# Sparse graph attention on one core: more slots in two chunks, the sum in the first slot's buffer, and ScalarE's first part put one or two tiles later

## The chip, the cores and the metric

The kernel runs on one core of a Trainium2 chip. The metric is the device time of one execution in microseconds (us). The core has five engines that work side by side: TensorE (PE, with its weight loads shown apart as PEld), VectorE (DVE), ScalarE (ACT), GpSimd (POOL) and SyncE (SP). The last three also issue transfers, which 16 DMA engines carry out. Each engine takes its instructions in a fixed order and waits on semaphores for the others.

## The reference

One layer of graph attention over N = 3327 nodes with D = 1024 features, with a residual. The adjacency is a dense int32 matrix, but almost all of it is zero.

```python
h = jnp.maximum(_layernorm(x, axis=-1), 0.0)
f = h @ Wf + bf
g = h @ Wg + bg
e = jax.nn.relu(f @ g.T)
scores = jnp.where(adj > 0, e, -9e15)
attention = jax.nn.softmax(scores, axis=1)
out = x + attention @ (h @ W + bW)
```

## The kernel before

The kernel does not compute all scores. **Part 1** reads the adjacency in 26 tiles of 128 rows, makes for each row a list of its neighbours (at most 40) and their number (the degree), writes the layer-normed rows h to DRAM (`hd`) and the lists to DRAM (`pd`), and builds A = Wf Wg^T, so that a row's scores against its neighbours are dots of q = h A with the neighbours' rows of h. Then the rows are ranked by degree, highest first, and `perm` holds the order. **Part 2** takes 128 ranked rows at a time. Such a group is called a slot s here, and `CAPS[s]` is how many neighbours its rows may have. For every k below the cap, one indirect transfer gathers 128 rows of h, each the k-th neighbour of its row.

```python
CAPS = [37, 25, 23, 22, 21, 21, 20, 20, 19, 19, 18, 18, 17, 17, 17, 16, 16, 15, 15, 15, 14, 14, 13, 13, 12, 11]
ONE_CHUNK = 20
AHEAD = 3
LAG = 4
```

Part 1, one tile. Odd tiles take their mean and variance on VectorE, even ones on ScalarE:

```python
def normed(t):
    ...                                   # xt: 128 rows of x, loaded
    if t % 2:
        ...                               # L406: two bn_stats, bn_aggr -> mv
        nc.scalar.activation(nmr[:n], mv[:n, 0:1], AF.Copy, scale=-1.0)            # L409
        nc.scalar.activation(rstd[:n], mv[:n, 1:2], AF.Sqrt, bias=eps[:n])         # L410
    else:
        ...                               # L414 to L418: the same with sums on ScalarE
    nc.vector.reciprocal(rstd[:n], rstd[:n])                                       # L419
    nc.scalar.activation(nmr[:n], nmr[:n], AF.Copy, scale=rstd[:n])                # L420
    nc.scalar.activation(xt[:n], xt[:n], AF.Relu, bias=nmr[:n], scale=rstd[:n])    # L421
    ...                                   # L423: xt stored to hd

def degrees(t):
    r = kpool.tile([P, N], FP, name="r")  # four buffers; the adjacency rows are loaded into it
    ...
        nc.scalar.activation(r[:n, b:e], a[:n, b:e], AF.Relu, accum_out=to)        # L435: 0/1 and degree
        nc.gpsimd.tensor_mul(r[:n, b:e], r[:n, b:e], iotaj[:n, b:e])               # L436: column numbers

def edges(t, r):
    cand = cpool.tile([P, SEG * 8], FP, name="cand")
    for s in range(SEG):                  # L446: the 8 largest of each of 16 segments
        nc.vector.max(cand[:n, s * 8 : s * 8 + 8], r[:n, s * SW : min(N, (s + 1) * SW)])
    pos = cpool.tile([P, SEG * 8], BF, name="pos")
    nc.vector.tensor_scalar(pos[:n], cand[:n], 0.0, None, op0=ALU.is_gt, op1=ALU.add,
                            accum_out=cnt[:n, t : t + 1])                          # L448: count
    for i in range(0, KM, 8):             # L452, L454: the 40 largest, in order
        nc.vector.max(lst[:n, i : i + 8], cand[:n])
        if i + 8 < KM:
            nc.vector.match_replace(cand[:n], lst[:n, i : i + 8], cand[:n], 0.0)
    nc.vector.tensor_scalar(lst[:n], lst[:n], float(N), 1.0, op0=ALU.min, op1=ALU.max)      # L455
    nc.vector.tensor_scalar(pay[:n, t, :KM], lst[:n], -1.0, None, op0=ALU.add)              # L456
    dg = cpool.tile([P, 1], FP, name="dg")
    nc.vector.tensor_scalar(dg[:n], deg[:n, t : t + 1], float(NBIN - 1), None, op0=ALU.min) # L458
    nc.vector.tensor_copy(pay[:n, t, KM : KM + 1], dg[:n])                                  # L459
    nc.vector.tensor_scalar(oh[:n, t, :], iotad[:n], dg[:n], None, op0=ALU.is_equal)        # L460

for t in range(NT):
    r = degrees(t)
    normed(t)
    edges(t, r)
    ...                                   # counts by degree, stores of lists, one of the 8 steps for A (L519)
```

Part 2. `prepare(s)` gathers the lists and rows of a slot and computes q (TensorE, L667). A slot above `ONE_CHUNK` is cut into two chunks, whose softmaxes are joined by rescaling the first sum.

```python
gpool = ctx.enter_context(tc.tile_pool(name="G", bufs=23))
ypool = ctx.enter_context(tc.tile_pool(name="y", bufs=2))

def dot(s, k):
    g = G[s, k] = gpool.tile([P, D], FP, name="G")
    gather(g, hd[:, :], e["pi"][:, k : k + 1])                # L638, POOL
    nc.vector.tensor_tensor_reduce(junk, g, q, ...)           # L684: one score per row

def softmax(s, k0, k1, last):
    ...                                   # L693 mask, L695 maximum
    if k0: ...                            # L697: joint maximum with the first chunk
    ...                                   # L699: exp and its sum
    if k0: ...                            # L702 and L703: factor al and joint sum
    if last: ...                          # L706 reciprocal, L708 al * rs (if k0), L709 sc * rs
    if k0:
        nc.scalar.activation(e["y"], e["y"], AF.Copy, scale=al)                    # L711

def on_tensor(s, k0, k1):                 # which k of the last chunk are summed on TensorE
    m = min(max(0, CAPS[s] - 13), k1 - k0 - 2)
    ...

def combine(s, k0, k1, last):
    if not k0:
        e["y"] = ypool.tile([P, D], FP, name="y")
    ...
        if k in pe:
            nc.scalar.activation(g, g, AF.Copy, scale=p)                           # L741
            sum_transposed(e, g, e["first"], False)                                # L725: 8 transposes
        elif k == 0:
            nc.scalar.activation(y, g, AF.Copy, scale=p)                           # L745
        else:
            nc.vector.scalar_tensor_tensor(y, g, p, y, op0=ALU.mult, op1=ALU.add)  # L747

def project(s): ...                       # y transposed, 16 matmuls with W (L759), copied to res (L761)

def finish(s):
    gather(e["r"], x[:, :], perm[:, s : s + 1], compute_op=ALU.add)                # res += x
    ins = nc.gpsimd.indirect_dma_start(out=out[:, :], ..., in_=e["r"], ...)        # L767: rows written out

for i, (s, k0, k1) in enumerate(units):   # units: the chunks in order
    last = k1 == CAPS[s]
    dots(s, range(k0, k1))
    if not k0 and s:
        finish(s - 1)
    softmax(s, k0, k1, last)
    if i + 1 < len(units):
        s2, a, b = units[i + 1]
        dots(s2, range(a, min(b, a + AHEAD)))
    combine(s, k0, k1, last)
    if last:
        project(s)
        if s + 2 < NT:
            prepare(s + 2)
```

The order of the instructions on each engine is made by the compiler's scheduler from this program order as a priority; it is not the order of the lines. A second, dense path runs only if a flag says that some row has more neighbours than its slot allows; it does not run with these inputs.

Of the kernel before, what the change touches and what calls it, by code (L numbers as in the profile page):

```python
# [8 lines left out]
FP = mybir.dt.float32  # L9
# [15 lines left out]
CAPS = [37, 25, 23, 22, 21, 21, 20, 20, 19, 19, 18, 18, 17, 17, 17, 16, 16, 15, 15, 15, 14, 14, 13, 13, 12, 11]  # L25
ONE_CHUNK = 20
AHEAD = 3
# [262 lines left out]
def edge_path(ctx: ExitStack, tc: tile.TileContext, x, adj, Wf, bf, Wg, bg, W, bW, out, flag):  # L290
# [45 lines left out]
    nc.gpsimd.memset(ones3, 1.0)  # L336
    bads = const.tile([P, NT + 2], FP, name="bads")
    nc.gpsimd.memset(bads, 0.0)
# [12 lines left out]
    with ExitStack() as part1:  # L351
# [3 lines left out]
        wT = pool1("wT", 2)  # L355
        ln = pool1("ln", 5)
        lnj = pool1("lnj", 1)
        kpool = pool1("key", 4)
        cpool = pool1("cand", 2)
        p_tr = pool1("p_tr", 2, space=PSUM)  # L360
# [32 lines left out]
        pre = p_c.tile([P, NBIN], FP, name="pre")  # L393

        def normed(t):

# [4 lines left out]
            rstd = ln.tile([P, 1], FP, name="rstd")  # L401
            nmr = ln.tile([P, 1], FP, name="nmr")
            if t % 2:
                st = ln.tile([P, D // CB, 6], FP, name="st")
                for c in range(D // CB):
                    nc.vector.bn_stats(st[:n, c, :], xt[:n, c * CB : (c + 1) * CB])  # L406
                mv = ln.tile([P, 2], FP, name="mv")
                nc.vector.bn_aggr(mv[:n], st[:n])
                nc.scalar.activation(nmr[:n], mv[:n, 0:1], AF.Copy, scale=-1.0)  # L409
                nc.scalar.activation(rstd[:n], mv[:n, 1:2], AF.Sqrt, bias=eps[:n])  # L410
            else:
                sums = ln.tile([P, 2], FP, name="sums")
                j = lnj.tile([P, D], BF, name="lnj")
                nc.scalar.activation(j[:n], xt[:n], AF.Copy, accum_out=sums[:n, 0:1])  # L414
                nc.scalar.activation(nmr[:n], sums[:n, 0:1], AF.Copy, scale=-1.0 / D)
                j = lnj.tile([P, D], BF, name="lnj")
                nc.scalar.activation(j[:n], xt[:n], AF.Square, bias=nmr[:n], accum_out=sums[:n, 1:2])
                nc.scalar.activation(rstd[:n], sums[:n, 1:2], AF.Sqrt, bias=eps[:n], scale=1.0 / D)  # L418
            nc.vector.reciprocal(rstd[:n], rstd[:n])  # L419
            nc.scalar.activation(nmr[:n], nmr[:n], AF.Copy, scale=rstd[:n])  # L420
            nc.scalar.activation(xt[:n], xt[:n], AF.Relu, bias=nmr[:n], scale=rstd[:n])  # L421
# [3 lines left out]
        def degrees(t):  # L425
# [13 lines left out]
            return r  # L439

        def edges(t, r):

            n = rows(t)
            cand = cpool.tile([P, SEG * 8], FP, name="cand")
            for s in range(SEG):
                nc.vector.max(cand[:n, s * 8 : s * 8 + 8], r[:n, s * SW : min(N, (s + 1) * SW)])  # L446
            pos = cpool.tile([P, SEG * 8], BF, name="pos")
            nc.vector.tensor_scalar(  # L448
                pos[:n], cand[:n], 0.0, None, op0=ALU.is_gt, op1=ALU.add, accum_out=cnt[:n, t : t + 1]
            )  # L450
            for i in range(0, KM, 8):
                nc.vector.max(lst[:n, i : i + 8], cand[:n])  # L452
                if i + 8 < KM:
                    nc.vector.match_replace(cand[:n], lst[:n, i : i + 8], cand[:n], 0.0)  # L454
            nc.vector.tensor_scalar(lst[:n], lst[:n], float(N), 1.0, op0=ALU.min, op1=ALU.max)  # L455
            nc.vector.tensor_scalar(pay[:n, t, :KM], lst[:n], -1.0, None, op0=ALU.add)  # L456
            dg = cpool.tile([P, 1], FP, name="dg")
            nc.vector.tensor_scalar(dg[:n], deg[:n, t : t + 1], float(NBIN - 1), None, op0=ALU.min)  # L458
            nc.vector.tensor_copy(pay[:n, t, KM : KM + 1], dg[:n])  # L459
            nc.vector.tensor_scalar(oh[:n, t, :], iotad[:n], dg[:n], None, op0=ALU.is_equal)  # L460

        def counted(t):
# [4 lines left out]
            nc.tensor.matmul(pre, tri, oh[:, t, :], start=(t == 0), stop=False, skip_group_check=True)  # L467
            hit = cpool.tile([P, NBIN], FP, name="hit")
            nc.vector.scalar_tensor_tensor(
# [84 lines left out]

        for t in range(NT):
            r = degrees(t)
            normed(t)
            edges(t, r)
            if t >= LAG:
# [7 lines left out]
            if t == 2 * KD:  # L567
                make_rows()
        for t in range(NT - LAG, NT):
            counted(t)  # L570
# [37 lines left out]
        nc.vector.tensor_copy(tens, ps[:, NT : 2 * NT])  # L608
        nc.vector.scalar_tensor_tensor(perm, ps[:, :NT], float(P), tens, op0=ALU.mult, op1=ALU.add)
        over = c1.tile([P, 1], FP, name="over")  # L610
# [5 lines left out]
        nc.vector.tensor_scalar(ne, deg, 1.0, None, op0=ALU.is_lt)  # L616
        nc.vector.tensor_reduce(bads[:, NT + 1 : NT + 2], ne, AX.X, ALU.max)


    W_sb = ctx.enter_context(tc.tile_pool(name="W", bufs=1)).tile([P, KD, O], FP, name="W_sb")  # L620
    nc.sync.dma_start(W_sb, W.rearrange("(k p) o -> p k o", p=P))
    psp = ctx.enter_context(tc.tile_pool(name="ps", bufs=3))
    gpool = ctx.enter_context(tc.tile_pool(name="G", bufs=23))
    hpool = ctx.enter_context(tc.tile_pool(name="hp", bufs=2))
    qpool = ctx.enter_context(tc.tile_pool(name="q", bufs=2))
    hTpool = ctx.enter_context(tc.tile_pool(name="hT", bufs=1))
    ypool = ctx.enter_context(tc.tile_pool(name="y", bufs=2))
    yTpool = ctx.enter_context(tc.tile_pool(name="yT", bufs=1))
# [8 lines left out]
    def gather(to, table, idx, **kw):  # L637
        nc.gpsimd.indirect_dma_start(  # L638
            out=to,
# [39 lines left out]
    def dot(s, k):  # L679
        e = st[s]  # L680
        g = G[s, k] = gpool.tile([P, D], FP, name="G")
        gather(g, hd[:, :], e["pi"][:, k : k + 1])
        junk = jpool.tile([P, D], BF, name="junk")
# [46 lines left out]
    def combine(s, k0, k1, last):  # L730
        e = st[s]
        if not k0:
            e["y"] = ypool.tile([P, D], FP, name="y")
        y = e["y"]
        e["first"] = True
        pe = on_tensor(s, k0, k1) if last else []
        for k in range(k0, k1):
# [6 lines left out]
            elif k == 0:  # L744
                nc.scalar.activation(y, g, AF.Copy, scale=p)  # L745
            else:
                nc.vector.scalar_tensor_tensor(y, g, p, y, op0=ALU.mult, op1=ALU.add)  # L747

    def project(s):
# [6 lines left out]
        for o in range(OH):  # L756
# [4 lines left out]
            nc.scalar.copy(r[:, o * CB : (o + 1) * CB], ps)  # L761

    def finish(s):
        e = st[s]

        gather(e["r"], x[:, :], perm[:, s : s + 1], compute_op=ALU.add)
        ins = nc.gpsimd.indirect_dma_start(  # L767
            out=out[:, :],
            out_offset=bass.IndirectOffsetOnAxis(ap=perm[:, s : s + 1] if s < N // P else final, axis=0),
            in_=e["r"],  # L770
            in_offset=None,
            bounds_check=None if s < N // P else N - 1,
            oob_is_err=s < N // P,
        )
        tc.declare_no_dep(ins.ins, group="results", reason="other rows")
# [27 lines left out]
    for i, (s, k0, k1) in enumerate(units):  # L803
        last = k1 == CAPS[s]
        dots(s, range(k0, k1))
        if not k0 and s:
            finish(s - 1)
        softmax(s, k0, k1, last)
        if i + 1 < len(units):
            s2, a, b = units[i + 1]  # L810
            dots(s2, range(a, min(b, a + AHEAD)))
        combine(s, k0, k1, last)
        if last:
# [46 lines left out]
```

## Time and profile before

| | us |
|---|---|
| median of 3 runs | 1418.14 (1415.55 to 1426.23) |
| profiled span | 1415.5, mean granted TensorE clock 0.927 |
| part 1: first to last MAX8 (L446) on VectorE | 20.7 to 267.1 |
| ranking and the first slot's q, until the first dot | 267 to 313 |
| last dot starts | 1353.2 |

In the profile's lines, an entry such as `L745` is the line of the kernel, `y<-G,sc` is the tile written and the tiles read, and `x26` is the number of instructions. A wait is written as the engine and instruction that stood still, an arrow, and what ended the wait. A gather's busy time on POOL is the time to issue it; the transfer itself is told by the DMA views, which give for G a median of 6.1 us from issue to landing.

### The profile page before, as it was taken

The page shows a single profiled execution, that of the slowest core. Times are in us where ns is not written, and L with a number is a line of the kernel's source. Part 1 is how long each engine was busy: PE and PEld are TensorE (multiplying, and loading weights), DVE is VectorE, ACT ScalarE, POOL GpSimd, SP SyncE. Part 2 cuts the span into 40 slices and gives each one's busy share as a digit, 9 for nine tenths or more (in the row PEclk, how much of TensorE's full clock was granted, in tenths as well). Part 3 has the DMA queues.
Part 4 walks back from the last instruction along what each step waited for, and adds up shares of the span by engine and source line. Part 5 has one row for each costly group of instructions (what it writes and reads, how often), then busy time and mean ns, then how long its engine had stood idle before and what let it go on. Part 6 is the DMA issues. An engine that isn't in the chain of part 4 may idle for free.

```text
span 1415.5 us, 14137 instructions
## 1 busy us (share of the span) xinstructions
PE 1172.8 (83%) x4355; PEld 684.0 (48%) x4355; DVE 1221.1 (86%) x2550; ACT 474.8 (34%) x738; POOL 876.6 (62%) x628
## 2 busy tenths in 40 slices
PE   4569998167288999999878977899999999999784
PEld 3544554044165556665545544555555555555331
DVE  4888889919979999998898788889999999999970
ACT  6666776311063244433312321222222222222110
POOL 8677777364666766775556556666667766666501
PEclk9999999578599999999989988999999999999897
DMA  9898796196678999886778667878889888888712
GB/s 370 330 356 307 294 346 229 49 361 236 227 269 289 316 315 330 282 291 224 266 284 277 192 248 265 275 233 266 256 285 304 273 265 255 256 285 286 242 31 61
DMA packets 97710, 372.52 MB, mean 263 GB/s; under 512 B 14268, under 2 KB 14684, under 8 KB 94297
## 3 DMA queue, kind: packets, MB, share of 16 engines
q0 software_dynamic: 79552, 286.85, 60.6%
q1 hardware_dynamic: 10860, 70.49, 13.2%
q10 hardware_dynamic: 7212, 14.18, 2.8%
q8 instruction: 36, 0.59, 0.2%
q14 instruction: 50, 0.41, 0.1%
HBM read 343.67 MB, written 27.80 MB: 262 GB/s over the span
## 4 chain that ended last, share of the span: by engine, by line
issue 26%; DVE 23%; PE 20%; POOL 18%; DMA 9%; ACT 4%; POOLq 0%; ACTq 0%; SPq 0%; DVEq 0%
DVE y L747 11%; POOL r L436 10%; PE ps_o L759 10%; POOL G L638 6%; DVE junk L684 6%; DMA G<-hd,pi 5%; PE ps_q L667 4%; PE yT_ps L725 3%; DMA pi<-pd,perm 2%; ACT G L741 2%; DVE cand L446 2%; PE ps_A L519 1%; DVE sc L684 1%; POOL res L638 1%; ACT r L435 1%
## 5 line engine op out<-in xcount | busy, mean ns | idle before, releaser
L638 POOL DMA_INDIRECT G<-hd,pi x468 | 542.8, 1160 | 260.0 <-issue 99.2
L684 DVE CUSTOM_DVE_ANT_0 junk<-G,q 128x1024 bf16<-128x1024 f32 x468 | 601.1, 1284 | 68.2 <-DMA G<-hd,pi 48.7
L667 PE MATMUL ps_q<-A_sb,hT 128*128 128x342 f32 x1248 | 394.2, 464 | 53.6 <-ACT q L669 43.2
L747 DVE SCALAR_TENSOR_TENSOR y<-G,sc,y 128x1024 f32<-128x1024 f32 x320 | 411.7, 1286 | 8.0 <-ACT y L745 6.1
L759 PE MATMUL ps_o<-W_sb,yT 128*128 128x512 f32 x832 | 387.6, 621 | 9.5 <-ACT yT L754 9.1
L667 PEld LDWEIGHTS ps_q<-A_sb,hT 128*128 128x128 f32 x1248 | 231.4, 193 | 172.3 <-ACT q L669 44.6
L759 PEld LDWEIGHTS ps_o<-W_sb,yT 128*128 128x128 f32 x832 | 161.2, 198 | 208.9 <-issue 190.6
L436 POOL TENSOR_TENSOR r<-r,iotaj 128x3327 f32<-128x3327 f32 (+4 forms) x28 | 188.6, 6740 | 67.0 <-ACT r L435 50.4
L446 DVE MAX8 cand<-r 128x8 f32<-128x208 f32 (+2 forms) x416 | 134.9, 363 | 35.2 <-POOL r L436 35.2
L741 ACT ACTIVATE G<-G,sc 128x1024 f32<-128x1024 f32 x122 | 129.8, 1137 | 0.0
L519 PE MATMUL ps_A<-WgT,WfT 128*128 128x512 f32 x256 | 120.7, 633 | 1.1 <-ACT WfT L490 1.0
L761 ACT COPY res<-ps_o 128x512 f32<-128x512 f32 x52 | 30.4, 585 | 269.2 <-PE ps_o L760 269.2
L725 PE MATMUL yT_ps<-ident,G 128*128 128x128 f32 x976 | 116.5, 275 | 3.2 <-ACT G L741 3.2
L725 PEld LDWEIGHTS yT_ps<-ident,G 128*128 128x128 f32 x976 | 107.0, 140 | 15.8 <-ACT G L741 7.9
L669 ACT COPY q<-ps_q 128x342 f32<-128x342 f32 x78 | 33.5, 450 | 199.3 <-DVE sc L684 94.4
L638 POOL DMA_INDIRECT res<-in_x_dram,perm x26 | 47.0, 1806 | 68.5 <-ACT res L761 65.4
L754 ACT COPY yT<-yT_ps 128x512 f32<-128x512 f32 x52 | 27.8, 587 | 166.4 <-PE yT_ps L725 166.4
L519 PEld LDWEIGHTS ps_A<-WgT,WfT 128*128 128x128 f32 x256 | 51.3, 203 | 65.0 <-issue 62.7
L725 PE MATMUL yT_ps<-ident,y 128*128 128x128 f32 x208 | 35.0, 323 | 52.3 <-DVE y L747 38.8
L435 ACT ACTIVATE r<-r 128x3327 f32<-128x3327 int32 (+4 forms) x28 | 77.5, 2766 | 0.1
L767 POOL DMA_INDIRECT out_dram<-res,perm x25 | 30.2, 1207 | 70.9 <-DMA res<-in_x_dram,perm 70.9
L651 ACT COPY hT<-ps_t 128x512 f32<-128x512 f32 x52 | 29.8, 592 | 117.6 <-PE ps_q L667 72.0
(139 smaller groups left out, 786.7 us busy)
## 6 DMA issues: line engine op xcount, KB each, us to landing
r<-in_adj_dram SPq DMA_DIRECT2D x25, 1663.5 KB, 9.6
xt<-in_x_dram SPq DMA_DIRECT2D x25, 512.0 KB, 10.2
hd<-xt ACTq DMA_DIRECT2D x25, 512.0 KB, 6.6
G<-hd,pi POOLq DMA_INDIRECT x468, 6.1
wr<-in_L_gnn_Wg_dram SPq DMA_DIRECT2D x8, 512.0 KB, 13.7
wr<-in_L_gnn_Wf_dram SPq DMA_DIRECT2D x8, 512.0 KB, 8.9
W_sb<-in_L_gnn_W_dram SPq DMA_DIRECT2D x1, 4096.0 KB, 16.6
r<-in_adj_dram SPq DMA_DIRECT2D x1, 1455.6 KB, 8.8
```

Source lines behind the costliest of these rows:

```text
L435: nc.scalar.activation(r[:n, b:e], a[:n, b:e], AF.Relu, accum_out=to)
L436: nc.gpsimd.tensor_mul(r[:n, b:e], r[:n, b:e], iotaj[:n, b:e])
L446: nc.vector.max(cand[:n, s * 8 : s * 8 + 8], r[:n, s * SW : min(N, (s + 1) * SW)])
L519: nc.tensor.matmul(ps, WfT[:, k, :], WgT[:, k, o * CB : (o + 1) * CB], start=(k == 0), stop=(k == KD - 1))
L638: nc.gpsimd.indirect_dma_start(out=to, out_offset=None, in_=table, in_offset=bass.IndirectOffsetOnAxis(ap=idx, axis=0), **kw,)
L667: nc.tensor.matmul(ps[:, :QB], hT[:, k, :], A_sb[:, k, o : o + QB], start=(k == 0), stop=False)
L669: nc.scalar.copy(q[:, o : o + QB], ps[:, :QB])
L684: nc.vector.tensor_tensor_reduce(junk, g, e["q"][:, :D], 1.0, e["q"][:, D : D + 1], op0=ALU.mult, op1=ALU.add, accum_out=e["sc"][:, k : k ...
L725: nc.tensor.matmul(e["yT"][:, c, :], g[:, c * P : (c + 1) * P], ident, is_transpose=True, start=(first and c % 4 == 0), stop=(last and c % ...
L741: nc.scalar.activation(g, g, AF.Copy, scale=p)
L747: nc.vector.scalar_tensor_tensor(y, g, p, y, op0=ALU.mult, op1=ALU.add)
L759: nc.tensor.matmul(ps, yT[:, k, :], W_sb[:, k, o * CB : (o + 1) * CB], start=(k == 0), stop=False)
```

## The change: what it does and what it is for

It has two parts. In part 2, slots with a cap of 17 to 20 are also worked in two chunks, so that gathers of one half can run while the other half is being summed. The sum y lives in the buffer of the slot's gather k = 0, which makes the pool `y` needless and leaves room for two more gather buffers. The gather that adds the residual is requested with the projection, and the write of the result comes behind the last gather requested by then.

In part 1, ScalarE's instructions that need a result of VectorE are moved one tile later (`scaled`, `stored`) or two (`kept`), so that the result is there when ScalarE comes to them. The count of candidates, the lists' conversion to int32 and the degree's copy go from VectorE to ScalarE. The one-hot row of the degree is made from the degree itself, without the minimum with 63; a new column of `bads` marks degrees of 64 and more, and `perm` is kept below N.

```diff
-ONE_CHUNK = 20
+ONE_CHUNK = 16
...
-        ln = pool1("ln", 5)
+        ln = pool1("ln", 6)
...
-        cpool = pool1("cand", 2)
+        cpool = pool1("cand", 4)
...
+        def scaled(t):
+            n = rows(t)
+            xt, rstd, nmr, *mv = lns[t]
+            if mv:
+                nc.scalar.activation(nmr[:n], mv[0][:n, 0:1], AF.Copy, scale=-1.0)
+                nc.scalar.activation(rstd[:n], mv[0][:n, 1:2], AF.Sqrt, bias=eps[:n])
             nc.vector.reciprocal(rstd[:n], rstd[:n])
+
+        def stored(t):
+            n = rows(t)
+            xt, rstd, nmr, *mv = lns.pop(t)
             nc.scalar.activation(nmr[:n], nmr[:n], AF.Copy, scale=rstd[:n])
             nc.scalar.activation(xt[:n], xt[:n], AF.Relu, bias=nmr[:n], scale=rstd[:n])
...
-            nc.vector.tensor_scalar(
-                pos[:n], cand[:n], 0.0, None, op0=ALU.is_gt, op1=ALU.add, accum_out=cnt[:n, t : t + 1]
-            )
+            rest = lnj.tile([P, SEG * 8], FP, name="rest")
+            of = cand
             for i in range(0, KM, 8):
-                nc.vector.max(lst[:n, i : i + 8], cand[:n])
+                nc.vector.max(lst[:n, i : i + 8], of[:n])
                 if i + 8 < KM:
-                    nc.vector.match_replace(cand[:n], lst[:n, i : i + 8], cand[:n], 0.0)
-            nc.vector.tensor_scalar(lst[:n], lst[:n], float(N), 1.0, op0=ALU.min, op1=ALU.max)
-            nc.vector.tensor_scalar(pay[:n, t, :KM], lst[:n], -1.0, None, op0=ALU.add)
-            dg = cpool.tile([P, 1], FP, name="dg")
-            nc.vector.tensor_scalar(dg[:n], deg[:n, t : t + 1], float(NBIN - 1), None, op0=ALU.min)
-            nc.vector.tensor_copy(pay[:n, t, KM : KM + 1], dg[:n])
-            nc.vector.tensor_scalar(oh[:n, t, :], iotad[:n], dg[:n], None, op0=ALU.is_equal)
+                    nc.vector.match_replace(rest[:n], lst[:n, i : i + 8], of[:n], 0.0)
+                    of = rest
+            ids = cpool.tile([P, KM], FP, name="ids")
+            nc.vector.tensor_scalar(ids[:n], lst[:n], float(N), 1.0, op0=ALU.min, op1=ALU.max)
+            found[t] = cand, ids
+            nc.vector.tensor_scalar(oh[:n, t, :], iotad[:n], deg[:n, t : t + 1], None, op0=ALU.is_equal)
+
+        def kept(t):
+            n = rows(t)
+            cand, ids = found.pop(t)
+            pos = lnj.tile([P, SEG * 8], BF, name="pos")
+            nc.scalar.activation(pos[:n], cand[:n], AF.Sign, accum_out=cnt[:n, t : t + 1])
+            nc.scalar.activation(pay[:n, t, :KM], ids[:n], AF.Copy, bias=-1.0)
+            nc.scalar.copy(pay[:n, t, KM : KM + 1], deg[:n, t : t + 1])
...
         for t in range(NT):
+            if t:
+                scaled(t - 1)
             r = degrees(t)
             normed(t)
+            if t:
+                stored(t - 1)
+            if t >= 2:
+                kept(t - 2)
             edges(t, r)
...
-    gpool = ctx.enter_context(tc.tile_pool(name="G", bufs=23))
+    gpool = ctx.enter_context(tc.tile_pool(name="G", bufs=25))
...
-            e["y"] = ypool.tile([P, D], FP, name="y")
+            e["y"] = G[s, 0]
...
-                nc.scalar.activation(y, g, AF.Copy, scale=p)
+                nc.scalar.activation(y, y, AF.Copy, scale=p)
...
     def project(s):
...
+        gather(r, x[:, :], perm[:, s : s + 1], compute_op=ALU.add)
+
     def finish(s):
-        gather(e["r"], x[:, :], perm[:, s : s + 1], compute_op=ALU.add)
-        ins = nc.gpsimd.indirect_dma_start(
...
+        with tc.issue_after(st["gathered"].ins):
+            ins = nc.gpsimd.indirect_dma_start(
...
         dots(s, range(k0, k1))
-        if not k0 and s:
-            finish(s - 1)
         softmax(s, k0, k1, last)
         if i + 1 < len(units):
             s2, a, b = units[i + 1]
             dots(s2, range(a, min(b, a + AHEAD)))
+        if last and s:
+            finish(s - 1)
         combine(s, k0, k1, last)
```

## The prediction, made before the changed kernel was built or run

> **What bounds the kernel now.** I read the page's busy shares first, then the waits of single stretches, then windows, and last the timeline of the engine that a wait named.
>
> ```profile
> PE 1172.8 (83%) x4355; PEld 684.0 (48%) x4355; DVE 1221.1 (86%) x2550; ACT 474.8 (34%) x738; POOL 876.6 (62%) x628
> ```
>
> VectorE (DVE) has the largest share, but 86% is an average. The times of the reciprocal of line 706, one per slot, give the borders of the slots, so I asked for the windows that they mark. The columns are: length, then busy us of PE, PEld, DVE, ACT and POOL, the granted TensorE clock, the DMA share and GB/s.
>
> ```profile
> 620.80:1037.60 416.80, 370.12 (x1404) 217.62 (x1403) 365.01 (x540) 114.89 (x171) 249.14 (x216) 0.93 0.77 257
> 20.70:267.10 246.40, 184.15 (x686) 112.55 (x685) 211.83 (x1024) 168.47 (x264) 181.25 (x27) 0.92 0.79 297
> ...
> 1037.60:1340.00 302.40, 287.93 (x970) 156.54 (x969) 295.21 (x433) 67.62 (x119) 204.82 (x162) 0.99 0.84 271
> ```
>
> In the last row, slots with caps of at most 16, DVE is busy 295.2 of 302.4 us (98%): nothing but less DVE work helps there. In 620.8 to 1037.6, which holds the dots of slots 6 to 15, DVE is idle for 416.8 - 365.0 = 51.8 us. In the first part (first to last MAX8) it is idle for 246.4 - 211.8 = 34.6 us. These two holes are what the change can fill. The waits of the middle stretch (here 640 to 1000; columns: total us, times, longest) name the reason:
>
> ```profile
> POOL G L638 <- ACT y L745: 54.5, 8, 10.6
> ...
> DVE junk L684 <- DMA G<-hd,pi: 36.8, 24, 3.5
> ...
> POOL out_dram L767 <- DMA res<-in_x_dram,perm: 22.8, 8, 4.2
> ```
>
> GpSimd (POOL) cannot issue the next gather because no G buffer is free until ScalarE has taken slot 0 of the chunk (line 745), and DVE then waits for the late gather. POOL's timeline shows one such spot (start, length, and the idle time before it in brackets):
>
> ```profile
> 733.50 1.01 POOL L638 DMA_INDIRECT hp<-hd,perm  x1 [0.31 <-issue]
> 744.52 1.86 POOL L638 DMA_INDIRECT G<-hd,pi  x1 [10.01 <-ACT y L745]
> ...
> 754.75 0.97 POOL L767 DMA_INDIRECT out_dram<-res,perm  x1 [1.73 <-DMA res<-in_x_dram,perm]
> 756.02 1.85 POOL L638 DMA_INDIRECT G<-hd,pi  x1 [0.30 <-issue]
> ```
>
> A chunk of 19 plus 3 gathers ahead fills the 23 buffers; they come free only when the combine begins, after all 19 dots and the softmax. POOL stands for 10.0 us, and just when it may run again, it also sits behind the residual's transfer before it writes out a result. For the first part the waits of 0 to 270 say:
>
> ```profile
> POOL r L436 <- ACT r L435: 50.4, 17, 6.0
> ...
> DVE cand L446 <- POOL r L436: 35.2, 15, 3.7
> ...
> ACT nmr L420 <- DVE rstd L419: 22.6, 9, 5.9
> ...
> ACT nmr L409 <- DVE mv L408: 15.1, 6, 3.9
> ```
>
> It is a ring: ScalarE waits in its queue for a tiny VectorE result, so the next tile's relu (line 435) is late, so POOL's multiply (436) is late, so VectorE's MAX8 is late.
>
> **What the Trainium skill says.** "Perfetto Trace Analysis", section Optimization Strategy, says that a repeating gap on the engine that should be saturated can mean too little memory for the next tile. The trace agrees: one gap per slot, and behind it POOL's wait for a buffer. The same page, Optimizing Scalar/DVE Operations, gives every small operation a fixed cost, larger on ScalarE than on VectorE for SBUF, and advises offloading when VectorE is saturated. The trace agrees: the 128x1 cast takes 148 ns on DVE (line 459) and a 128x1 activation takes 198 ns on ACT (line 415); ACT has the room. Its section DMA Instruction — SWDGE (GPSIMD) says that a gather's profiled time is descriptor generation and not the data: here 942 ns on POOL (median) against 6.1 us to landing, so a late issue costs DVE several microseconds. "TensorE: Matmul & The Clock Gate", What's actually happening, says that idle time lowers the array's clock. Here the granted clock is 0.93 in the stretch with holes and 0.99 in the full one, so I take the lower clock there as a consequence of the holes.
>
> **The change, part by part.**
>
> *Two chunks above 16.* Slots 6 to 14 (caps 20, 20, 19, 19, 18, 18, 17, 17, 17), nine in number, are now cut in two. What a cut adds on DVE, from the groups by form: line 693 0.17, 695 0.16, 697 0.16, 703 0.22 and 708 0.16 us, together 0.87; nine make 7.8 us. The choice of slots for TensorE (the term cap - 13) gives the same number as before for each of these caps (7 for 20, 4 for 17), so neither the 1286 ns multiply-adds nor the transposes change in number. On ACT each cut adds a rescaling of y (1.15 us), two small exponentials and a read of the sum, about 2 us, beside an engine that is busy 115 of 417 us. What a cut takes away is the wait: half of the buffers come free while the other half's gathers are landing. How full DVE then gets I take from the slots that are cut already: in 440 to 480, 480 to 520, 520 to 560 and 560 to 600 it is busy 39.86, 39.89, 39.90 and 38.53 of 40 us, or 158.2/160 = 98.9%. So the stretch becomes (365.0 + 7.8)/0.989 = 377 us: **39.8 us less**.
>
> A cross-check from another view: in the timeline a dot followed by a dot starts every 1.33 us, and a dot with a multiply-add takes 2.42 us as a pair. A slot with cap 20 has 12 such pairs and 8 dots alone, 12 x 2.42 + 8 x 1.33 = 39.7, with small operations some 41 us. The reciprocals of slots 6, 7 and 8 now lie 45.2 and 47.8 us apart.
>
> *The sum in slot 0's buffer, G 25 instead of 23.* The memory is the same (two y buffers of the same size go). The buffer of k = 0 is no longer free after line 745, so the first free one comes one multiply-add (1.3 us) later. I put this at zero.
>
> *The residual's gather at the projection, the result's scatter behind the next gathers.* POOL's wait for the residual is 75.7 us in 26 times on the whole run. It matters only where DVE is short of gathers, and that is already counted. Zero.
>
> *First part.* Off VectorE go line 448 (6.9 + 2.1 us with its read), 456 (4.6), 458 (3.2) and 459 (3.7): **20.5 us of DVE**. On ScalarE come Sign with a sum, a copy of 40 and a copy of 1. By like rows (0.3 + 0.19, 0.3, 0.2 us) I estimate 1 us a tile, 26 in all, beside 168 of 246 us busy; and most of its waits for DVE (22.6 + 15.1 + 10.9 for the dg in front of line 409, some 49 us) should go, since it asks a tile later. VectorE would need 211.8 - 20.5 = 191.3 us. POOL's multiplies are 188.6 us in all. The transfers of this part are 80.7 MB, which at the best rate of the DMA view of that part (425 GB/s) take 190 us. Three floors at 190 lie under a stretch of 246 us, and a ring of four r buffers over load, relu, multiply and MAX8 will not run at all three. Low case: only 8 us appear, because transfers get in the way. High case: all 20.5 and half of the 34.6 us idle, 38. I take **22 us**, near the middle.
>
> *Ranking chain.* One more small operation before perm: +0.2 us. The two that fill the new column of flags lie behind it.
>
> Sum: 1418.1 - 39.8 - 22 + 0.2 = **1356.5 us**.
>
> **Rivals.** *TensorE takes over in the cut slots.* For: it is busy 370 of 417 us there. Against: that counts pipelined time. From the chain in order of time, 16 matmuls of line 667 take 4.87 us, 16 of line 759 take 7.06 and 64 transposes 6.99. A cap of 20 needs 3 x 4.87 + 2 x 7.06 + 72 x 0.109 for transposes, and some 1.7 for the rest, 38 us at full clock, under the 41 of VectorE. At a clock of 0.90 it would be 42 or 43, and half of the 39.8 would be lost: about 1375.
>
> *POOL gets a new wait.* The residual's gather now stands early in POOL's queue and needs the projection's end; POOL waited 65.4 us for ACT's res already. If it blocks gathers behind it for 5 us a slot, the two buffers more do not cover that, and up to 20 us come back: 1370 to 1380.
>
> *The first part is bound by transfers.* For: the DMA share in the first 50 us is about 1. Against: it is 0.79 over the stretch. If so the first part gives 8 us or less: 1370.
>
> *Better than thought.* If ScalarE is never late, the first part gives 38 us: 1340.
>
> **Range and chances.** One rival alone leaves 1370 to 1380; two together 1385; the good case with tidier slots 0 to 5 1335. Hence 1335 to 1385. Within 2% begins at 1389.8: it needs both gains to fail by more than half, for which I see 6 in 100, and 2 in 100 for slower.
>
> **What would show it.** Right: DVE idle in slots 6 to 15 falls from 52 to about 5 us; the wait of G on y (67.1 us) and of the dots on G (48.7 us) nearly go; that stretch lasts 377 us and its clock rises above 0.95; the last MAX8 ends near 245 us instead of 267; POOL's wait for ACT's relu halves. Wrong: a large wait of POOL for ACT res, or of PE on nothing but its own queue, in the cut slots; or gaps before MAX8 that a late adjacency transfer ends. The tail from 1340 (75 us, two projections in a row) and the start (267 to 345 us) I expect to stay; were the gain to come from there, the reasons above would be wrong.

## The result, and the profile after

The changed kernel takes 1378.15 us (median of 4 runs, 1373.38 to 1382.63) against 1416.85 us of the kernel before in the same runs: a ratio of 0.971 (95% interval 0.966 to 0.977). The time lies in the predicted range, 22 us above the predicted 1356.5 us.

The busy shares from the page of the changed kernel:

```profile
PE 1155.6 (84%) x4355; PEld 676.8 (49%) x4355; DVE 1220.0 (89%) x2468; ACT 505.3 (37%) x878; POOL 872.1 (64%) x628
```

VectorE's busy time is what it was (1221.1 us before), although it has 82 instructions fewer. The gain is idle time that went. The marks used in the prediction say where (us from the start of each profile; "s" is the reciprocal of a slot, on line 706 before and 744 after):

| mark | before | after | difference of the stretch |
|---|---|---|---|
| last MAX8 ends | 267.4 | 271.1 | +3.7 |
| first dot starts | 313.0 | 316.5 | -0.2 |
| s = 0 | 390.3 | 397.2 | +3.4 |
| s = 5 | 620.8 | 627.6 | -0.1 |
| s = 15 | 1037.6 | 996.3 | -48.2 |
| s = 25 | 1360.5 | 1316.4 | -2.8 |
| end | 1415.5 | 1371.7 | +0.3 |

So slots 6 to 15 gave more than was predicted (48.2 instead of 39.8 us), and the first part gave nothing: it got 3.7 us longer instead of 22 shorter.

The windows of the first part and of slots 6 to 15 in the changed kernel (columns as before: length, busy us of PE, PEld, DVE, ACT, POOL, granted clock, DMA share, GB/s):

```profile
20.70:271.10 250.40, 185.85 (x694) 113.56 (x692) 214.61 (x909) 182.28 (x363) 181.53 (x27) 0.93 0.80 293
627.60:996.30 368.70, 357.23 (x1420) 211.44 (x1419) 362.09 (x590) 130.60 (x208) 256.57 (x216) 1.00 0.88 296
```

In the slots, VectorE now stands for 368.7 - 362.1 = 6.6 us instead of 51.8, and the granted clock is 1.00 instead of 0.93. In the first part VectorE is busy for 214.6 us (before 211.8), and the stretch is longer.

POOL's timeline in the cut slots shows what the second chunk does (start, length, idle time before and what ended it):

```profile
765.00 1.74 POOL L676 DMA_INDIRECT G<-hd,pi  x1 [0.59 <-DVE G L785]
767.41 1.74 POOL L676 DMA_INDIRECT G<-hd,pi  x1 [0.67 <-DVE G L785]
769.81 1.74 POOL L676 DMA_INDIRECT G<-hd,pi  x1 [0.66 <-DVE G L785]
772.21 1.74 POOL L676 DMA_INDIRECT G<-hd,pi  x1 [0.66 <-DVE G L785]
```

There is still a wait for a buffer in front of each gather, but it is 0.7 us and not 10: each multiply-add (line 785, 747 before) frees one buffer, and the next gather starts at once. The starts lie 2.4 us apart, which is the pace of a dot and a multiply-add on VectorE. POOL now follows VectorE. VectorE's own waits on the whole run say the same: its wait for the gathers was 48.7 us before.

```profile
DVE junk L722 <- DMA G<-hd,pi: 13.8, 13, 4.2
```

The waits of the first part, 0 to 271 us:

```profile
POOL r L450 <- ACT r L449: 50.0, 17, 4.2
DVE cand L462 <- POOL r L450: 31.0, 23, 2.5
...
ACT nmr L434 <- DVE rstd L428: 24.2, 16, 4.2
...
ACT A_sb L545 <- PE ps_A L542: 14.9, 10, 4.1
```

POOL's wait for the relu is 50.0 us (before 50.4), and ScalarE's wait for the reciprocal is 24.2 us (before 22.6): the results that were to be ready one tile later are not. The timeline of all engines from 108 to 128 us, with other instructions left out, shows why:

```profile
108.93 7.28 POOL L450 TENSOR_TENSOR r<-r,iotaj 128x3327 f32<-128x3327 f32 x1 [2.61 <-ACT r L449]
...
116.24 0.38 DVE L462 MAX8 cand<-r 128x8 f32<-128x208 f32 x1 [2.46 <-POOL r L450]
...
121.17 0.14 DVE L428 RECIPROCAL rstd<-rstd 128x1 f32<-128x1 f32 x1
121.34 0.29 ACT L434 ACTIVATE nmr<-nmr,rstd 128x1 f32<-128x1 f32 x1 [2.57 <-DVE rstd L428]
...
124.53 2.96 ACT L449 ACTIVATE r<-r 128x3327 f32<-128x3327 int32 x1
...
127.66 7.26 POOL L450 TENSOR_TENSOR r<-r,iotaj 128x3327 f32<-128x3327 f32 x1 [1.53 <-ACT r L449]
```

VectorE's queue (its instructions in their fixed order) holds the reciprocal behind the 16 MAX8 of a tile, and these wait for POOL. ScalarE's queue holds the next relu behind the consumer of that reciprocal, and POOL waits for the relu. Start to start: multiply until the first MAX8 7.3 us, MAX8 until the reciprocal 4.9, step to ScalarE 0.2, ScalarE's work until the relu 3.2, relu until the multiply 3.1, together 18.7 us. In this time one more multiply runs, so a tile takes 9.4 us, and 26 of them 244 of the stretch's 250 us. This was my theory after the result, **R, the ring**. Its rival, **D**, was that VectorE's own serial work fills a tile's period. A third thought, **F**, was that the small operations taken from VectorE had only filled gaps there.

### The profile page after: what moved, and what is told of

Read it like the earlier page. It is cut to its first block, busy times and chain, and to the rows that moved or that the text cites. A ratio compares the mean times of both kernels' runs of the same rounds, so it can differ in the third digit from the quotient of the medians.

```text
span 1371.7 us, 14152 instructions
## 1 busy us (share of the span) xinstructions
PE 1155.6 (84%) x4355; PEld 676.8 (49%) x4355; DVE 1220.0 (89%) x2468; ACT 505.3 (37%) x878; POOL 872.1 (64%) x628
## 4 chain that ended last, share of the span: by engine, by line
PE 36%; issue 18%; DVE 13%; POOL 6%; DMA 5%; ACT 2%; POOLq 0%; DVEq 0%; ACTq 0%
PE ps_q L705 15%; PE ps_o L797 14%; DVE G L785 7%; POOL G L676 5%; PE yT_ps L763 4%; DMA G<-hd,pi 4%; DVE junk L722 4%; DMA pi<-pd,perm 1%; PE ps_q L706 1%; DVE sc L722 1%; PE ps_o L798 1%; ACT hT L689 1%; ACT G L779 1%; DMA hp<-hd,perm 1%; PE ps_t L688 1%
## 5 line engine op out<-in xcount | busy, mean ns | idle before, releaser
L676 POOL DMA_INDIRECT G<-hd,pi x468 | 536.5, 1146 | 219.6 <-DVE G L785 92.9
L785 DVE SCALAR_TENSOR_TENSOR G<-G,sc 128x1024 f32<-128x1024 f32 x320 | 410.7, 1284 | 4.6 <-ACT G L783 4.0
L797 PE MATMUL ps_o<-W_sb,yT 128*128 128x512 f32 x832 | 374.1, 603 | 3.9 <-ACT yT L792 3.8
L797 PEld LDWEIGHTS ps_o<-W_sb,yT 128*128 128x128 f32 x832 | 156.3, 192 | 194.4 <-issue 182.1
L763 PE MATMUL yT_ps<-ident,G 128*128 128x128 f32 x1184 | 146.4, 279 | 26.2 <-DVE sc L747 8.1
L763 PEld LDWEIGHTS yT_ps<-ident,G 128*128 128x128 f32 x1184 | 133.9, 143 | 43.3 <-issue 15.5
L462 DVE MAX8 cand<-r 128x8 f32<-128x208 f32 (+2 forms) x416 | 123.1, 360 | 31.0 <-POOL r L450 31.0
L676 POOL DMA_INDIRECT res<-in_x_dram,perm x26 | 45.8, 1762 | 67.2 <-ACT res L799 62.7
L542 PEld LDWEIGHTS ps_A<-WgT,WfT 128*128 128x128 f32 x256 | 51.2, 203 | 68.1 <-issue 61.4
L807 POOL DMA_INDIRECT out_dram<-res,perm x25 | 35.2, 1407 | 74.4 <-DMA res<-in_x_dram,perm 74.4
L676 POOL DMA_INDIRECT hp<-hd,perm x26 | 29.9, 1149 | 34.2 <-DVE final L649 20.2
L688 PE MATMUL ps_t<-ident,hp 128*128 128x128 f32 x208 | 31.2, 292 | 16.7 <-issue 10.2
## 6 DMA issues: line engine op xcount, KB each, us to landing
r<-in_adj_dram SPq DMA_DIRECT2D x25, 1663.5 KB, 10.1
```

Source lines behind the costliest of these rows:

```text
L542: nc.tensor.matmul(ps, WfT[:, k, :], WgT[:, k, o * CB : (o + 1) * CB], start=(k == 0), stop=(k == KD - 1))
L676: return nc.gpsimd.indirect_dma_start(out=to, out_offset=None, in_=table, in_offset=bass.IndirectOffsetOnAxis(ap=idx, axis=0), **kw,)
L688: nc.tensor.transpose(ps[:, k, :], of[:, (g + k) * P : (g + k + 1) * P], ident)
L763: nc.tensor.matmul(e["yT"][:, c, :], g[:, c * P : (c + 1) * P], ident, is_transpose=True, start=(first and c % 4 == 0), stop=(last and c % ...
L797: nc.tensor.matmul(ps, yT[:, k, :], W_sb[:, k, o * CB : (o + 1) * CB], start=(k == 0), stop=False)
```

## The experiments

Every kernel but the last computes the whole reference. "Kernel 1" and so on are the numbers of the experiments. The runs of all sets but the one of the woven kernels were made on chips where every kernel ran some 3% slower and less steadily (the kernel before took 1461 to 1462 us there, 1420 us in the woven set), so whole times are compared within a set only; the marks of the first part repeat there (262.4 to 263.7 us in three kernels with the old first part, 270.3 to 270.9 in two with the new one). The old first part took until 267.4 us in the profile above, so what the new one costs is 3 to 9 us.

**1. The border alone.**

```diff
 # kernel before
-ONE_CHUNK = 20
+ONE_CHUNK = 16
```

> The kernel before with only the border moved from 20 to 16 (y keeps its own pool, G keeps 23 buffers, residual and scatter as before, first part as before). Theory A (the two chunks alone close the holes): the reciprocals of slots 5 and 15 lie about 370 us apart (changed kernel 368.6, before 416.9), whole time about 1370 us. Rival B (the two more buffers or the moved residual gather are needed too): the stretch stays above 390 us, whole time above 1388 us.

Measured: 1433.2 us, ratio 0.990 (0.973 to 1.006); from slot 5 to slot 15 it takes 389.2 us, 28 less than the 416.9 of the kernel before on a faster chip. Kernel 3, which keeps the border at 20, ran in the same set and takes 438.4 us there (in a run 13 us above its median). The window and two waits of these slots in kernel 3, then the window and the one of these waits that is left in kernel 1:

```profile
651.38:1089.76 438.38, 370.24 (x1401) 218.10 (x1400) 365.55 (x542) 114.52 (x171) 251.38 (x217) 0.92 0.74 248
POOL G L677 <- ACT y L784: 68.0, 9, 13.9
DVE junk L723 <- DMA G<-hd,pi: 36.8, 24, 4.7
```

```profile
643.84:1033.00 389.16, 362.65 (x1417) 211.80 (x1416) 362.20 (x589) 130.58 (x208) 259.26 (x215) 0.98 0.84 279
POOL G L638 <- ACT y L745: 5.4, 2, 4.1
```

POOL's wait for the first buffer and VectorE's wait for the gathers go with the border alone. VectorE still stands for 27 us of the stretch on this chip; the whole changed kernel does for 22 us on a slow chip (384.5 - 362.4 in kernel 5) and for 6.6 us on the faster one.

**2. The whole second part with the first part of before** (everything before the load of W from the old kernel, everything behind from the new one), in the same set.

> The first part of the kernel before with the whole second part of the changed one. If the first part's changes cost time, as the marks of the changed trace say (reciprocal of slot 0 at 397.2 us against 390.3), this is faster than the changed kernel by 3 to 7 us: about 1372 us, reciprocal of slot 0 near 391 us. If the later start of slot 0 comes from the second part's changes (y in slot 0's buffer), it starts at 394 us or later in this kernel too and nothing is gained.

Measured: 1437.1 us, ratio 0.995 (0.983 to 1.008); from slot 5 to slot 15 it takes 390.1 us. Neither of the absolute times of the expectations could be met on this chip, and 389 lies at the rival's border of 390. In whole time neither kernel 1 nor kernel 2 is shown to be faster than before in this set, since both intervals take in 1. But side by side the two kernels take the same time for the slots: with the border moved, the two buffers, y in slot 0's buffer and the moved residual add nothing in that stretch. That fits the whole run's waits of POOL for the residual's transfer, which did not fall (75.7 us before, 79.2 after). The last MAX8 ends at 263.4 us.

From slot 15 to slot 25, where the border changes nothing, the two kernels do differ: 341.6 us with the border alone and 324.8 here. On the faster chip the same stretch took 322.9 us before and 320.1 after. So the other pieces of the second part may be worth more on a slower chip; the whole times of kernels 1 and 2 do not show it, and no run separates the pieces.

From the first dot to the reciprocal of slot 0 this kernel takes 79.7 us, the one with only the border 76.6; before it was 77.3 and in the changed kernel 80.7. So the 3 us that slot 0 lost belong to the second part. Which of its three pieces costs them stays open.

**3. The new first part alone**, with the second part of before and the border at 20.

> The changed first part with the second part of before (border 20). Theory: no gain, last MAX8 near 270.7 us (before 267.1), whole time 1415 to 1424 us. The prediction on record had 22 us less: 1395 us. A time at or under 1405 would mean that the first part's gain exists and something in the second part took it away.

Measured: 1472.8 us, ratio 1.018 (1.003 to 1.033); last MAX8 ends at 270.9 us, against 263.7 and 263.4 in the two kernels above. The new first part ends later with the old second part too, so its gain was not there to be taken away later.

**4. The relu one tile ahead.**

```diff
 # changed kernel
+        ahead = degrees(0)
         for t in range(NT):
...
-            r = degrees(t)
+            r = ahead
+            if t + 1 < NT:
+                ahead = degrees(t + 1)
             normed(t)
```

> The changed kernel, but the relu and the multiply of tile t + 1 stand ahead of the other work of tile t in program order. Theory R (a ring: MAX8, reciprocal, ScalarE's chain, next relu, multiply, MAX8): POOL's wait for ACT's relu falls from 50 us to under 20, last MAX8 by 255 us, whole time about 1362 us. Rival D (VectorE itself is the bound: its serial chain of max and replace fills the tile's period): POOL then waits for buffers that VectorE holds instead, last MAX8 stays at 265 to 271, no gain. Rival T (the transfers are the bound): waits for the adjacency's load appear on ScalarE.

Measured: 1419.6 us, ratio 0.984 (0.973 to 0.995); last MAX8 ends at 254.4 us, 16.5 us before kernel 3. The waits of its first part:

```profile
POOL r L450 <- ACT r L449: 42.1, 13, 8.1
...
ACT nmr L434 <- DVE rstd L428: 7.4, 5, 2.6
```

ScalarE's wait for the reciprocal falls to 7.4 us. POOL's wait for the relu is 42.1 us, not under 20. There is no wait worth naming for the adjacency's load apart from the first one (8.0 us), so transfers are not the bound here. VectorE is busy 214.7 of 234.7 us.

**5 and 6. The changed kernel again, and kernel 2 beside it.**

> The changed kernel once more, as the base of this set. 1373 to 1383 us if the chip is undisturbed, ratio to the kernel before 0.97.

> The first part of before with the second part of the changed kernel, beside the changed kernel. If the changed first part costs time: last MAX8 ends at 263 to 267 us against 271, whole time 3 to 8 us under the changed kernel in this set. If the first parts are equal: within 2 us.

Measured: the changed kernel 1417.5 us, ratio 0.969 (0.959 to 0.978); the other 1430.2 us, ratio 0.978 (0.971 to 0.986). The last MAX8 ends at 270.3 and 262.4 us, 8 us apart as theory R says, but the whole times stand the other way round, with intervals that overlap: from the last MAX8 to the first dot one takes 51.2 and the other 64.1 us, where the two profiles of the faster chip have 45 to 46. I can't tell a few microseconds of whole time on this chip; the comparison is inconclusive.

**7. The relu ahead in the first part of before**, counts and casts still on VectorE, with the new second part.

```diff
 # first part of before
+        ahead = degrees(0)
         for t in range(NT):
-            r = degrees(t)
+            r = ahead
+            if t + 1 < NT:
+                ahead = degrees(t + 1)
             normed(t)
             edges(t, r)
```

> The first part of before (counts and casts on VectorE, reciprocal and store in their old places), with only relu and multiply one tile ahead in program order, and the changed second part. Theory R and F (the ring is cut at the relu, and VectorE's small operations fall into the gaps of its own serial chain): last MAX8 ends near 254 us as with the relu ahead in the changed kernel. Rival (the operations taken from VectorE are worth their 20 us once the ring is cut): last MAX8 ends at 265 us or later.

Measured: 1407.2 us, ratio 0.953 (0.941 to 0.965); last MAX8 ends at 246.4 us. That is 16 to 17 us earlier than in kernels 2 and 6, whose relu is in its old place, and 8 us earlier than in kernel 4, which has none of the small operations on VectorE. Kernels 4 and 7 differ also in the places of ScalarE's instructions, so the 8 us belong to all of these moves together; in any case taking 20.5 us off VectorE gave no gain.

**8. The removed operations done on VectorE as well.**

```diff
 # changed kernel
+            pos2, cnt2, pay2, dg2 = ...       # scratch, read by nothing
+            nc.vector.tensor_scalar(pos2[:n], cand[:n], 0.0, None, op0=ALU.is_gt, op1=ALU.add, accum_out=cnt2[:n])
...
+            nc.vector.tensor_scalar(pay2[:n, :KM], ids[:n], -1.0, None, op0=ALU.add)
+            nc.vector.tensor_scalar(dg2[:n], deg[:n, t : t + 1], float(NBIN - 1), None, op0=ALU.min)
+            nc.vector.tensor_copy(pay2[:n, KM : KM + 1], dg2[:n])
```

> The changed kernel with the operations that were taken off VectorE done there as well, into scratch tiles that nothing reads (count, minus one with cast, minimum, cast of the degree). Theory F (they fill gaps): last MAX8 ends within 4 us of the changed kernel's 271, VectorE's busy time in the first part rises by less than 6 us. The step of the prediction on record (20.5 us of VectorE): last MAX8 some 15 to 20 us later, near 288.

Measured: 1451.5 us, ratio 1.004 (0.999 to 1.009); last MAX8 ends at 294.4 us, 24 us later, and VectorE is busy for 250.2 us, 35 more. Theory F falls in this form: here the operations do cost time. The waits of this kernel from 0 to 300 us show where:

```profile
POOL r L450 <- ACT r L449: 81.0, 19, 11.9
...
ACT nmr L434 <- DVE rstd L428: 48.8, 16, 10.2
```

Both waits of the ring have grown (from 50.0 and 24.2 us), which fits that the operations stand in VectorE's queue and lengthen the ring. The scheduler also gave the other operations of VectorE new places (489 of 914 up to the last MAX8), so the 24 us are those of this kernel and not of the added operations alone.

The kernel before has these operations on VectorE too, with the relu in the same place, and there VectorE is busy for 212.2 us and not 250.2. What differs is the order on VectorE. Two places of its timeline, first the kernel before, then the changed one:

```profile
149.87 0.15 DVE L458 TENSOR_SCALAR dg<-deg 128x1 f32<-128x1 f32 x1
149.94 0.29 DVE L448 TENSOR_SCALAR_CACHE_REDUCE pos<-cand 128x128 bf16<-128x128 f32 x1
...
150.15 0.30 DVE L452 MAX8 held<-cand 128x8 f32<-128x128 f32 x1
150.35 0.15 DVE L459 CAST pay<-dg 128x1 int32<-128x1 f32 x1
150.48 0.10 DVE L454 MATCH_VALUE_LOAD cand<-held,cand 128x8 f32 x1
```

```profile
130.71 0.30 DVE L466 MAX8 held<-cand 128x8 f32<-128x128 f32 x1
131.05 0.10 DVE L468 MATCH_VALUE_LOAD rest<-held,cand 128x8 f32 x1
```

From a maximum to the next step of its chain it is 0.33 us with a cast in between and 0.34 without: the step waits for the maximum's result, and the cast is free. In the profile of before, 196 of the 416 MAX8 over segments stand alone between other operations of VectorE (233 in kernel 7); in the changed kernel 65 do (76 in kernel 8). The scheduler ordered the changed kernel so that a tile's chain mostly runs by itself.

**9 and 10. Two tiles woven on VectorE**, without and with the relu ahead.

```diff
 # changed kernel (9), kernel 4 (10)
             for s in range(SEG):
-                nc.vector.max(cand[:n, s * 8 : s * 8 + 8], r[:n, ...])
+                ins = nc.vector.max(cand[:n, s * 8 : s * 8 + 8], r[:n, ...])
+                with tc.issue_after(ins.ins):
+                    next(old, None)           # one operation of the chain of tile t - 1
```

> The changed kernel, but VectorE's serial chain of a tile (max and replace, 11 operations) is issued in turn with the 16 MAX8 of the next tile, one by one, in a forced order. Theory I (what the change lost is the interleaving of two tiles on VectorE): VectorE's busy time in the first part falls from 215 us to 185 to 195, last MAX8 ends by 258. Theory R (the ring through the reciprocal is the bound): the reciprocal now stands behind a woven stretch of 8 us instead of 4.5, ScalarE waits longer for it, and the last MAX8 ends at 270 or later although VectorE is busy for less.

> The same with relu and multiply one tile ahead in program order. If both theories hold, each for its share: busy time of VectorE as in the woven kernel, POOL's wait for ACT's relu under 30 us, last MAX8 by 245 us (relu ahead alone 254); ratio to the kernel before about 0.95. If only the relu's place mattered: 254 again.

Measured for the woven kernel: 1384.0 us, ratio 0.975 (0.972 to 0.978). VectorE's busy time falls to 197.5 us, 17 less, and the last MAX8 ends at 279.4 us, 8 later. The waits of its first part:

```profile
DVE cand L484 <- POOL r L450: 58.7, 19, 5.3
POOL r L450 <- ACT r L449: 50.6, 14, 8.2
ACT nmr L434 <- DVE rstd L428: 44.2, 15, 5.8
```

This separates the theories: VectorE is busy for much less and the stretch grows, while ScalarE's wait for the reciprocal, which now stands behind a longer block, grows from 24.2 to 44.2 us. Being busy (D) was not the bound; the order was.

With the relu ahead: **1350.8 us** (1346.4 to 1352.5), ratio 0.951 (0.948 to 0.955); last MAX8 ends at 246.4 us, VectorE busy for 196.5 us. These are 33 us less than without it, in the whole time as in the first part, and the forced turns of chain and MAX8 on VectorE are the same in both. POOL's wait for the relu is 30.9 us and was expected under 30:

```profile
POOL r L450 <- ACT r L449: 30.9, 14, 5.1
...
ACT nmr L434 <- DVE rstd L428: 10.1, 8, 3.2
```

**11. The same weaving with the count and casts on VectorE** (kernel 7, woven).

> The relu ahead, the count and casts on VectorE as in the kernel before, woven in the same forced order, with the changed second part. If small operations on VectorE cost next to nothing once another tile's MAX8 stand between them: last MAX8 within 5 us of the woven kernel with relu ahead. If they cost their 20 us of durations: 15 us later or more. Without weaving this kernel ended its last MAX8 at 246.4 us, so 240 to 250 here.

Measured: 1353.9 us, ratio 0.952 (0.949 to 0.955); last MAX8 ends at 250.2 us, 3.8 us after kernel 10, VectorE busy for 210.2 us. Its ScalarE instructions also keep their old places, so these 4 us are what all moves of the new first part are worth together in this order; in whole time the intervals overlap.

**12. The reciprocal left out.** ScalarE scales by the deviation itself and waits for nothing of VectorE there; this kernel leaves a step of the layer norm out.

```diff
 # changed kernel
-            nc.vector.reciprocal(rstd[:n], rstd[:n])
```

> The changed kernel without the reciprocal of line 428 (26 operations of 0.15 us on VectorE, so ScalarE scales by the deviation and not by its inverse; this leaves a step of the computation out, ScalarE's order of instructions stays the same). Theory R (the ring through the reciprocal): ScalarE's 24 us of waiting for it go, POOL's wait for ACT's relu falls from 50 us to under 35, last MAX8 ends by 260 us against 271, which is far more than the 4 us of work left out; ratio to the kernel before 0.963 or less. Rival (ScalarE's own 182 us of work and its waits for TensorE make the relu late): the wait stays near 50 us, last MAX8 at 266 to 271, ratio 0.97.

Measured: 1432.1 us, ratio 0.982 (0.970 to 0.993); last MAX8 ends at 267.0 us, only 4 us earlier, as much as the work left out. The waits of the first part:

```profile
POOL r L449 <- ACT r L448: 51.6, 17, 9.3
...
ACT A_sb L544 <- PE ps_A L541: 29.6, 9, 6.4
```

Theory R, as I had put it, missed here. The wait for the reciprocal is gone, and the multiplies come earlier up to the thirteenth tile's (at 120.2 instead of 127.7 us in the changed kernel). Then another wait takes its place:

```profile
126.54 0.59 ACT L544 COPY A_sb<-ps_A 128x512 f32<-128x512 f32 x1 [6.41 <-PE ps_A L541]
134.77 7.27 POOL L449 TENSOR_TENSOR r<-r,iotaj 128x3327 f32<-128x3327 f32 x1 [7.33 <-ACT r L448]
```

ScalarE stands for 6.4 us for TensorE's product in a step for A, the relu stands behind that, and POOL stands for 7.3 us. On the first part ScalarE's wait for these products, 14.9 us in the changed kernel, doubles. The expectation took ScalarE's order as unchanged, and it is not: up to the last MAX8, 240 of its 369 instructions that both kernels have stand in another place, by up to 15 places. So how much one wait alone is worth stays open. What the kernel shows is that the reciprocal was one of several waits in ScalarE's queue ahead of the next relu.

The first parts side by side (us; waits up to the last MAX8):

| kernel | last MAX8 ends | VectorE busy / stretch | POOL for relu | ScalarE for reciprocal | ScalarE for A |
|---|---|---|---|---|---|
| before | 267.4 | 212.2 / 246.8 | 50.4 | 22.6 | 16.4 |
| changed | 271.1 | 214.6 / 250.4 | 50.0 | 24.2 | 14.9 |
| 8, operations doubled | 294.4 | 250.2 / 273.8 | 81.0 | 43.6 | 10.5 |
| 9, woven | 279.4 | 197.5 / 258.9 | 50.6 | 44.2 | 8.2 |
| 12, no reciprocal | 267.0 | 215.8 / 246.6 | 51.6 | none | 29.6 |
| 4, relu ahead | 254.4 | 214.7 / 234.7 | 42.1 | 7.4 | 22.6 |
| 10, woven, relu ahead | 246.4 | 196.5 / 226.4 | 30.9 | 10.1 | 23.1 |
| 7, before with relu ahead | 246.4 | 210.7 / 226.9 | 36.5 | 10.2 | 12.1 |

All four kernels with the relu ahead (the fourth is 11) end 8 us or more before any without (254.4 at the latest, against 262.4 at the earliest in kernel 6). Between kernels that differ by this alone in their first part it is 16.5 us (4 against 3), 16 to 17 (7 against 2 and 6) and 33 (10 against 9). Where the scheduler chose VectorE's order, that order changed with it. In the kernels without the relu ahead, the end does not follow VectorE's busy time (9 has the least and ends late).

## Why the prediction was right or wrong

*The bound before, and the wait behind it* were read rightly. The hole in the cut slots was the missing buffer, and the border alone takes both waits away (kernel 1 against 3). One count was off: in the trace, four gathers of the next slot and not three are issued before POOL stands (19 + 4 = 23).

*The step (365.0 + 7.8)/0.989 = 377 us* was right in mechanism and 8 us too large, since the stretch took 368.7. The term +7.8 for the five small operations of nine cuts does not show: VectorE's busy time in the stretch fell from 365.0 to 362.1. Part of the reason is in the prediction's own cross-check: a dot and a multiply-add in turn take 2.42 us, while a dot after a dot starts 1.33 us later and a multiply-add after a multiply-add 1.32. More turns make the same work shorter. POOL's four starts above, 2.4 us apart, are such turns. That this makes up the whole difference is argued and not shown.

*The clock* rose to 1.00, as expected of a stretch without holes; TensorE is busy for 97% of it and was for 89%. The Trainium skill ("TensorE: Matmul & The Clock Gate", section What's actually happening) says that the clock follows how busy TensorE has been, and the trace agrees. TensorE did not take over (357 of 368.7 us busy, VectorE idle for 6.6).

*POOL's waits* were partly misread. I expected the wait for a buffer nearly to go. It moved to the multiply-adds (92.9 us in 91 times on the whole run) and is harmless there, since what counts is VectorE's wait for the gathers, which fell from 48.7 to 13.8 us. The new wait that a rival feared, POOL for ScalarE's `res`, did not come: 62.7 us on the whole run, 65.4 before.

*The first part* is where the prediction failed, in three of its steps.

- "20.5 us of DVE" was a sum of profiled durations. VectorE's busy time did not fall (211.8 to 214.6 us from first to last MAX8). The Trainium skill ("Perfetto Trace Analysis", Optimizing Scalar/DVE Operations) says that the write-acknowledgement half of an operation's fixed cost, which the profiled duration includes, overlaps with the next instruction. The trace agrees, and I had not applied it: one MAX8 takes 0.36 us, 16 in a row 4.52 us, or 0.28 each, and the small operation of line 458 above lasts 0.15 us while the next one starts after 0.07. Beyond that, a cast in the gap of a serial chain costs nothing (0.33 and 0.34 us above), and where little other work stands between the steps the same operations add to VectorE's busy time (kernel 8: 35 us, with the last MAX8 24 us later; that this is their full duration each is not shown). So the estimate of what VectorE needs, 191.3 us, was wrong as well; only the two woven kernels without these operations get near it (196.5 and 197.5).
- "Most of its waits for DVE should go, since it asks a tile later" did not hold. The waits for mean and degree in front of line 409 did go (15.1 + 10.9 to 3.6 + 0.5 us), but the one for the reciprocal stayed (22.6 to 24.2), because the scheduler put the reciprocal behind the MAX8 of the tile between. A later place in program order is not a later place than the producer's on its own engine.
- "Three floors at 190" was no bound of this stretch. The order in ScalarE's queue was: the relu that feeds POOL stood behind the waits of the tile before. Moving the relu ahead gains 16.5 us (4 against 3); kernel 12, without one of the waits, ends 4 us earlier than the changed kernel. What bounds the first part once the relu is ahead, at 246 us, stays open.

The low case of the first part (8 us) was still too good, and no rival named a change of order made by the scheduler. The rival of transfers was wrong: the DMA share stays at 0.80, and ScalarE waits for no load after the first.

*Range.* 39.8 + 22 was predicted and 48.2 - 3.7 came, less 3.4 lost in slot 0 and with 2.8 gained later. The slots gave 8 us more than predicted and the first part 26 less; that the time still fell into the range is in part luck, since the two errors partly cancelled.

## What to carry to other kernels

When operations move between engines that work in order, find where their producers and the next tile's first step stand in the queues; put the step that feeds the longest chain ahead of everything that may wait. Do not sum the durations of small operations: see in the timeline whether they stand in the gap of a serial chain or lengthen it. And when a pool of buffers is emptied only at the end of a batch, halving the batch can take the wait away without any more buffers (kernel 1; more buffers without the halving were not tried).

## What the runs showed of the hardware that was not expected

Weaving two independent chains lowered VectorE's busy time for the same operations from 214.6 to 197.5 us, although the number of instructions hardly changed (909 and 908). And the doubled operations of kernel 8, whose durations in the kernel before add up to 20.5 us, came with 35 us more of busy time.
